# A four-layer graph network on one core: f1 rows by head in the encoder, more kept attention tiles, pair sums in tiles of their own

## Chip, core and metric

The kernel runs on one core of a Trainium2 chip. The metric is the device time in microseconds. An engine is named as the profile names it: PE is the matmul engine (PEld its weight loads), DVE the vector engine, ACT the engine of the activation functions, POOL the GpSimd engine, SP the engine that here only issues transfers. SP and ACT can issue transfers through the hardware queue, POOL through the software queue.

## What is computed

Four layers of a graph network over N = 2708 nodes with 512 features; each ends in a layer norm of its input plus its result. The change lies in the first layer (heads H = 4, width D = 128) and touches one product that the fourth layer uses. Of the reference:

```python
Xw = jnp.einsum('hnd,hde->hne', Xh, W)
f1 = jnp.einsum('hnd,hd->hn', Xw, V[:, 0, :, 0])
f2 = jnp.einsum('hnd,hd->hn', Xw, V[:, 1, :, 0])
sig = jax.nn.sigmoid(f1[:, :, None] + f2[:, None, :])
att = _masked_softmax(pattern[None] * sig, mask)      # local and long-range pattern are both adj
Xa = jnp.einsum('hij,hjd->hid', att, Xw)
Xn = _batchnorm(Xc, enc_bn_gamma, enc_bn_beta)
emb = _mlp_block(Xn, enc_mlp_W, enc_mlp_b, enc_mlp_bn_gamma, enc_mlp_bn_beta)
Y = jnp.einsum('hij,hjd->hid', att, Yh)               # Yh: emb by heads
Y = jnp.einsum('hnd,hed->hne', Y, W)
out = _mlp_block(jax.nn.elu(Yc), dec_mlp_W, ...)
```

The same attention matrix is thus used twice: on Xw (called the encoder here) and on emb (the decoder). Layer 2 needs the number of neighbours of each node. Layer 4 is a softmax attention with projections Wq and Wk; the kernel multiplies the two weight matrices once (called mqk) and applies the product.

## The kernel before

**Attention passes.** The attention matrix is never stored whole. `attention_pass` runs once for the encoder (`first` is true) and once for the decoder. It goes over two halves of the query nodes (`hf` 0 and 1, 1354 columns each) and, in each, over two pairs of heads (`p` 0 and 1): eight passes in all. A pass goes over the 22 blocks of 128 key nodes in the order `ORDER`; a block's number in that order is its place. The block with only 20 nodes stands at place 11.

**One step.** `form` makes the tile `t` (128 keys x 2 heads x 1354 queries) of a block: two tanh on ACT (L400), one for each head, from the row of f1 spread over all partitions (tile `f1b`) and the keys' f2 as bias; one operation on DVE that masks it with the adjacency block `a` (L408); one exponential on ACT (L409). PE then multiplies it with the values into six PSUM banks `po` (L478; a float32 matmul shows as two records, so a step has twelve). Tiles `t` have four buffers, adjacency blocks four in the encoder and three in the decoder.

**Encoder.** In passes with p = 0 the adjacency block is read from the input, changed so that missing edges become a large negative number (L389 and L390, with the single tile `z`), and written to `adj_d` from POOL (L394). All later passes read `adj_d`. The encoder also needs the sums of the exponentials over the keys: PE multiplies `t` with a block of ones into PSUM `psm` (L507). With p = 0, and at the first four and last two places, each tile is summed alone. At the other places with p = 1, DVE first adds the second tile of a pair to the first, in place (L498), and PE sums that. This is written as `add_up`, which is kept in `waiting` and called in the next step, before that step's matmuls; its add is ordered behind the next step's masking with `tc.issue_after`.

**Kept tiles.** The tiles at the places of `KEPT[p]` are written to memory by the encoder (L457, from POOL) and loaded by the decoder (L460, from SP) instead of being formed again.

**Counts.** For layer 2, `count` (L350, DVE) counts the missing edges of every block once in each half, in the decoder: with p = 0 where the block is formed there, with p = 1 where it is kept for p = 0. If a block is kept for both, it is loaded for the count alone. In `form` the count is written ahead of the tanh.

**f1 rows.** `f1b` holds both heads of a pass in one tile with two buffers, so the next pass's rows can be loaded while one runs (L427, SP).

**Between the passes.** At the end of a pass `finish` empties the six PSUM banks (encoder: copies L598 on ACT and DVE; decoder: `take`, L846 on DVE), and the rest of the work on the result is spread over the steps of the next pass.

**Weights of layer 4.** Between encoder and decoder, `merged(c)` makes block c of mqk with four matmuls of 512 columns (L699); two of the four blocks are made there, and the transposed weights go to memory. The other two are made after the decoder (L985, copied by L993, stored from POOL by L994), while the last batch norm is computed.

The text is not the order of the queues. The framework plans each engine's instructions by its own estimate of times, with the text's order as priority and `tc.issue_after(x)` as an edge to an instruction on the same engine.

## Time and profile before

| what | us |
|---|---|
| three runs | 3268.78, 3267.47, 3268.74 (median 3268.74) |
| the profiled execution | 3272.62 |
| its span, first to last instruction | 3270.8 |

In the profiled execution the first matmul of the eight passes starts at these times (us from the start of the span): encoder 44.4, 174.0, 298.6, 432.8; decoder 670.2, 778.4, 887.8, 1017.3. The encoder's last matmul ends at 556 and the decoder's last `po` matmul at 1121; between the two lie batch norm and MLP. Layer 2 of the reference starts with the first `tp_out` at 1186, its large product at 1277, and the two softmax layers take the span from 1493 on.

How to read it: the profile's lines give line, engine and tiles; a line "A <- B: x, n, y" of the waits says that A stood still x us in total, n times, at most y, until B was done. In the table by stretches each engine's busy time is followed by its number of instructions; then come the granted PE clock, the share of DMA time and GB/s. A busy PE can still run below its full rate, so the length of a step is to be compared too: twelve records of L478 take 4.55 us at full rate.

Rows of the groups that the change touches:

| operation | count, mean |
|---|---|
| L400 tanh, 1354 columns | 312, 1413 ns |
| L409 exponential, 2708 columns | 156, 2453 ns |
| L408 masking, 2708 columns | 156, 2976 ns |
| L498 pair add, 2708 columns | 14 whole ones, 2975 ns |
| L350 count, 1354 columns | 42 whole ones, 1560 ns |
| `a` from `adj_d` | 110 loads of 677 KB |
| `t` to and from memory | 16 stores and 16 loads of 1354 KB, besides those of the short block |
| `f1b` | 8 loads of 1354 KB |

### The profile page before, as it was taken

To read this page: it belongs to the slowest core of one execution; us is meant where nothing else is said; L and a number is where in the kernel's file an instruction comes from. 1 tells how busy PE (TensorE), PEld (TensorE's weight loads), DVE (VectorE), ACT (ScalarE), POOL (GpSimd) and SP (SyncE) were. 2 spreads that over 40 slices of the span, in tenths; PEclk is the share of its full clock that TensorE was granted. 3 is DMA by queue.
4 is the path that set the end of the run, shared out by engine and by line. 5 is a ranking of instruction groups with operands and counts; after the bars stand their busy time and mean duration, and the time that the engine had idled before them with its cause. 6 is when DMAs were issued, how large, how long until landed. Compare 5 with 4: busy or idle time off the path is not lost.

```text
span 3270.8 us, 30357 instructions
## 1 busy us (share of the span) xinstructions
PE 3212.9 (98%) x10906; PEld 1717.4 (53%) x10906; DVE 1944.1 (59%) x3144; ACT 1346.8 (41%) x1512; POOL 132.9 (4%) x215
## 2 busy tenths in 40 slices
PE   8999999999999999999999999999999999999999
PEld 5444444444444446885555555544455555555554
DVE  7878977867687685445136666777353442543433
ACT  6888886567868652001133434443021020110211
POOL 1100100000000000000010000000000000000000
PEclk9999999999999999999999999999999999999999
DMA  7856854245545412550034444553211111111100
GB/s 278 314 187 223 298 200 147 88 152 194 169 163 177 169 53 80 144 133 15 1 118 136 118 124 137 151 160 111 72 47 32 45 35 37 41 34 45 35 24 20
DMA packets 173158, 384.59 MB, mean 118 GB/s; under 512 B 21034, under 2 KB 115190, under 8 KB 168334
## 3 DMA queue, kind: packets, MB, share of 16 engines
q1 hardware_dynamic: 157214, 309.74, 31.1%
q0 software_dynamic: 15792, 72.91, 5.9%
q8 instruction: 86, 1.41, 0.2%
q14 instruction: 66, 0.54, 0.1%
HBM read 308.79 MB, written 73.24 MB: 117 GB/s over the span
## 4 chain that ended last, share of the span: by engine, by line
PE 87%; DVE 6%; ACT 3%; DMA 2%; issue 1%; SPq 0%; DVEq 0%; ACTq 0%
PE po L1377 23%; PE po L478 18%; PE ps_s L1256 17%; PE ps_nb L1109 7%; PE ps_wide L1158 4%; PE psm L507 3%; DVE t L408 2%; PE ps_hid L129 2%; PE ps_sup L1554 2%; PE ps_o L1485 2%; PE ps_dec L880 2%; ACT t L400 2%; ACT t L409 1%; PE ps_mlp L755 1%; DMA a<-adj_d 1%
## 5 line engine op out<-in xcount | busy, mean ns | idle before, releaser
L408 DVE SCALAR_TENSOR_TENSOR t<-t,a 128x2708 f32<-128x2708 f32 (+1 forms) x156 | 462.4, 2976 | 135.2 <-ACT t L400 131.2
L400 ACT ACTIVATE t<-f1b,f2h 128x1354 f32<-128x1354 f32 (+1 forms) x312 | 427.2, 1413 | 63.5 <-PE psm L507 32.1
L409 ACT ACTIVATE t<-t 128x2708 f32<-128x2708 f32 (+1 forms) x156 | 382.2, 2453 | 95.0 <-DVE t L408 94.8
L478 PE MATMUL po<-t,xw 128*128 128x452 f32 (+3 forms) x1056 | 412.9, 553 | 7.7 <-ACT t L409 7.7
L478 PE MATMUL po<-t,emb 128*128 128x452 f32 (+3 forms) x1056 | 403.1, 550 | 12.5 <-ACT t L409 9.2
L1256 PE MATMUL ps_s<-sup,hT 128*128 128x384 f32 (+1 forms) x1176 | 407.4, 490 | 0.0
L1377 PE MATMUL po<-sup,e 128*128 128x512 f32 x882 | 407.1, 595 | 0.2 <-DVE xs L1613 0.2
L1377 PE MATMUL po<-e,xs 128*128 128x384 f32 (+1 forms) x1176 | 406.0, 489 | 0.0
L1688 DVE SCALAR_TENSOR_TENSOR e<-a_cols,ps_s 128x384 f32<-128x384 f32 (+1 forms) x154 | 85.7, 556 | 450.4 <-PE ps_s L1256 427.5
L1256 PEld LDWEIGHTS ps_s<-sup,hT 128*128 128x128 f32 x1176 | 221.8, 190 | 164.2 <-issue 14.2
L478 PEld LDWEIGHTS po<-t,emb 128*128 128x128 f32 (+1 forms) x1056 | 194.9, 192 | 213.6 <-issue 189.2
L1377 PEld LDWEIGHTS po<-e,xs 128*128 128x128 f32 x1176 | 222.2, 190 | 160.2 <-issue 5.8
L478 PEld LDWEIGHTS po<-t,xw 128*128 128x128 f32 (+1 forms) x1056 | 189.1, 191 | 219.9 <-issue 199.9
L1377 PEld LDWEIGHTS po<-sup,e 128*128 128x128 f32 x882 | 160.3, 190 | 159.8 <-issue 136.9
L1256 PE MATMUL ps_s<-hT 128*128 128x384 f32 (+5 forms) x672 | 211.3, 461 | 1.4 <-DVE e L1604 0.8
L1355 ACT ACTIVATE e<-e 128x384 f32<-128x384 f32 (+1 forms) x308 | 151.9, 522 | 116.6 <-DVE e L1354 113.7
L1603 ACT ACTIVATE a_cols<-a_cols,neg_big 128x384 f32<-128x384 f32 (+1 forms) x154 | 94.5, 616 | 232.3 <-DMA a_cols<-in_adjT_dram 187.2
L1109 PE MATMUL ps_nb<-hid_hi,at 128*128 128x512 f32 x484 | 185.5, 390 | 0.4 <-DVE at L1101 0.4
L109 ACT ACTIVATE ln_rstd<-ln_rstd 128x1 f32<-128x1 f32 (+1 forms) x88 | 17.2, 201 | 395.9 <-DVE ln_rstd L108 395.4
L1109 PE MATMUL ps_nb<-hid_lo,at 128*128 128x512 f32 x462 | 180.1, 390 | 0.0
L1354 DVE TENSOR_TENSOR e<-e,nmax 128x384 f32<-128x384 f32 (+1 forms) x308 | 163.8, 555 | 23.3 <-ACT nmax L1347 23.3
L1256 PEld LDWEIGHTS ps_s<-hT 128*128 128x128 f32 x672 | 123.1, 190 | 90.2 <-issue 19.1
(252 smaller groups left out, 3321.0 us busy)
## 6 DMA issues: line engine op xcount, KB each, us to landing
a<-adj_d SPq DMA_DIRECT2D x110, 677.0 KB
a_cols<-in_adjT_dram SPq DMA_DIRECT2D x378, 192.0 KB
a<-in_adjT_dram SPq DMA_DIRECT2D x42, 677.0 KB
adj_d<-a POOLq DMA_DIRECT2D x42, 677.0 KB, 5.8
raw<-in_adjT_dram SPq DMA_DIRECT2D x105, 256.0 KB
kept<-t POOLq DMA_DIRECT2D x16, 1354.0 KB, 6.7
t<-kept SPq DMA_DIRECT2D x16, 1354.0 KB
a_cols<-in_adjT_dram SPq DMA_DIRECT2D x63, 202.0 KB
```

Source lines behind the costliest of these rows:

```text
L400: nc.scalar.activation(tv[:, k, :], f1b[:n, k, :w], AF.Tanh, bias=f2h[:n, jt, h : h + 1], scale=0.5,)
L408: step = nc.vector.scalar_tensor_tensor(tv, tv, GUARD, ab, ALU.add, ALU.mult)
L409: nc.scalar.activation(tv, tv, AF.Exp, scale=0.5)
L478: nc.tensor.matmul(po[HB * k + q][:, :qw], values[r : r + n, jt, h * P : (h + 1) * P], t[r : r + n, k, q0 : q0 + qw], start=(place == 0), ...
L507: nc.tensor.matmul(sums[k][32 * r : 32 * r + 32, :SW], ones32[:m], whole[:m, k, q0 + qw - SW : q0 + qw], start=first_one, stop=last_one,)
L1109: nc.tensor.matmul(pos[it][:n], at, half[:, jt, :], start=(jt == 0 and k == 0), stop=(jt == NT - 1),)
L1158: nc.tensor.matmul(ps[:, :width], w(c, o), xt(c), start=(c == 0), stop=(c == C - 1),)
L1256: nc.tensor.matmul(ps[:, b * P : w], keys[:, c, j0 : j0 + P], st["q"][:, c, b * P :], start=(c == 0), stop=(c == C - 1),)
L1354: nc.vector.tensor_tensor(e, e, st["nmax"][:, :w], ALU.add)
L1355: nc.scalar.activation(e, e, AF.Exp)
L1377: nc.tensor.matmul(out, lhsT, rhs, start=(k == 0), stop=(k == NT - 1))
L1603: nc.scalar.activation(a, a, AF.Identity, bias=neg_big[: a.shape[0]], scale=1.0e30)
```

## The change

Six things are changed. The words that go with the change speak of the decoder's f1 rows in tiles of two heads and of three adjacency buffers there; both are so in the kernel before as well, and stay.

1. `KEPT[1]` has eight places instead of five, so in each half three more tiles are stored by the encoder and loaded by the decoder. The places 4, 11 and 14 are now kept for both p; before, 11 alone.
2. `count` in `form` stands behind the exponential and is ordered behind the masking of its own step.
3. The pair sums: no `waiting`; the add follows its own step. It is made in two operations, one for each head, into tiles of their own ("z" and "pair", one buffer each). For the short block it is still made in place.
4. The encoder's f1 rows are in tiles of one head with three buffers. The second head's are loaded from ACT's queue.
5. `merged` makes three of four blocks between encoder and decoder, and one is left for after the decoder.
6. That last block is stored from SP instead of POOL.

```diff
-    KEPT = [(4, 8, 11, 14, 18), (3, 7, 11, 15, 19)]
+    KEPT = [(4, 8, 11, 14, 18), (1, 4, 7, 9, 11, 14, 17, 20)]
...
-    wqT_d = dram.tile([P, C, C // 2 * P], F32, name="wqT_d")
+    wqT_d = dram.tile([P, C, P], F32, name="wqT_d")
...
-            stage = att.tile([P, HP, HW], F32, tag="f1b", name="f1_rows", bufs=2)[:, 0, :]
-            f1b = att.tile([P, HP, HW], F32, tag="f1b", name="f1b", bufs=2)
+            stage, *f1b = [
+                att.tile([P, HW], F32, tag="f1b", name=name, bufs=HP + 1)
+                for name in ["f1_rows"] + ["f1b"] * HP
+            ]
...
-            spread = nc.sync.dma_start(
-                f1b[:, :, :w], f1_d[:HP, h0 : h0 + w].partition_broadcast(P)
-            )
+            for k in range(HP):
+                spread = nc.sync.dma_start(
+                    f1b[k][:, :w], f1_d[k, h0 : h0 + w].partition_broadcast(P)
+                )
...
-                if not first and p == (jt in KEPT[0]):
-                    count(hf, jt, att, a)
...
                 nc.scalar.activation(tv, tv, AF.Exp, scale=0.5)
+                if not first and p == (jt in KEPT[0]):
+
+                    with tc.issue_after(step.ins):
+                        count(hf, jt, att, a)
                 return step
...
-                        f1b = att.tile([P, HP, HW], F32, tag="f1b", name="f1b", bufs=2)
...
+                        if first:
+
+                            f1b = [
+                                att.tile([P, HW], F32, tag="f1b", name="f1b", bufs=HP + 1)
+                                for k in range(HP)
+                            ]
+                            with early:
+                                nc.sync.dma_start(f1b[0][:, :w], f1[:, 0, :])
+                            nc.scalar.dma_start(f1b[1][:, :w], f1[:, 1, :])
+                        else:
+                            both = att.tile([P, HP, HW], F32, tag="f1b", name="f1b", bufs=2)
+                            f1b = [both[:, k, :] for k in range(HP)]
+                            with early:
+                                nc.sync.dma_start(both[:, :, :w], f1)
...
-                        if waiting is not None:
-                            waiting(step)
-                            waiting = None
...
-                            if more is not None:
-                                with tc.issue_after(behind.ins):
-                                    nc.vector.tensor_tensor(
-                                        whole[: more.shape[0], :, :w],
-                                        whole[: more.shape[0], :, :w],
-                                        more,
-                                        ALU.add,
-                                    )
...
-                            waiting = partial(add_up, before, P, tv, False, False)
+                            whole, m = [], P
+                            for k, tag in enumerate(("z", "pair")):
+                                both = att.tile([P, HW], F32, tag=tag, name="pair", bufs=1)
+                                nc.vector.tensor_tensor(
+                                    both[:, :w], before[:, k, :w], tv[:, k, :], ALU.add
+                                )
+                                whole.append(both)
...
-            nc.gpsimd.dma_start(wqT_d, wqT[:, :, half * P :])
-            merged(1)
+            nc.gpsimd.dma_start(wqT_d, wqT[:, :, (C - 1) * P :])
+            for c in range(1, C - 1):
+                merged(c)
...
-                    for c in range(half):
-                        for o in range(C):
-                            nc.tensor.matmul(
-                                po[1 + c],
-                                wq_again[:, o, c * P : (c + 1) * P],
...
+                    for o in range(C):
+                        nc.tensor.matmul(
+                            po[1],
+                            wq_again[:, o, :],
...
-                for c in range(half):
-                    nc.scalar.activation(mqk[:, c, :], po[1 + c], AF.Copy, scale=qscale)
-                    nc.gpsimd.dma_start(
-                        mqk_d[:, :, half + c, :].rearrange("o p i -> p o i"),
+                nc.scalar.activation(mqk, po[1], AF.Copy, scale=qscale)
+                nc.sync.dma_start(
+                    mqk_d[:, :, C - 1, :].rearrange("o p i -> p o i"),
```

## The prediction

> **What bounds the kernel now.** I read the engine totals first, then the stretches by stage, then the waits of the two attention stretches, and last the chain and the PE timeline around the longest PE stalls.
>
> ```profile
> PE 3212.9 (98%) x10906; PEld 1717.4 (53%) x10906; DVE 1944.1 (59%) x3144; ACT 1346.8 (41%) x1512; POOL 132.9 (4%) x215
> ...
> 204.00:356.00 152.00, 147.98 (x623) 65.12 (x622) 134.10 (x83) 133.24 (x82) 10.65 (x19) 0.99 0.64 225
> ...
> 566.00:676.00 110.00, 106.50 (x335) 51.21 (x334) 89.06 (x140) 48.93 (x63) 2.92 (x4) 1.00 0.27 94
> 676.00:790.00 114.00, 106.12 (x286) 52.09 (x286) 74.50 (x59) 88.93 (x58) 1.06 (x2) 0.97 0.56 190
> 790.00:890.00 100.00, 96.17 (x258) 47.16 (x257) 65.68 (x45) 82.77 (x54) 0.00 (x0) 0.98 0.52 173
> 890.00:1000.00 110.00, 110.00 (x294) 54.46 (x293) 90.55 (x95) 74.89 (x55) 0.00 (x0) 0.98 0.48 165
> ```
>
> PE is the bound: 98% of the span and in no stage far from full. In the decoder all of 890 to 1000 is PE work. So an edit that relieves ACT, DVE or DMA is worth only what PE stands still for their sake, and an edit that moves PE work is worth what stands still where it left and where it arrives. Now those standstills, waits of ACT, DVE and PE, encoder (180 to 305, then PE in 180 to 556) and decoder (670 to 1121):
>
> ```profile
> ACT t L400 <- PE psm L507: 6.6, 4, 2.6
> ...
> PE po L478 <- ACT t L409: 7.7, 8, 2.3
> PE psm L507 <- DVE t L498: 2.8, 2, 1.4
> ...
> DVE z L350 <- DMA a<-adj_d: 30.1, 13, 4.2
> ...
> ACT t L409 <- DVE t L408: 71.0, 39, 5.8
> ...
> PE po L478 <- ACT t L409: 9.2, 7, 5.8
> PE po L478 <- DVE ot L846: 3.1, 1, 3.1
> ```
>
> The decoder chain is: DVE's zero count L350 stands ahead of a masking L408 whose tanh is done, and waits 30.1 us in all for its adjacency block; ACT's exponentials wait 71.0 us for L408; PE waits 9.2 us for ACT and 3.1 us for the DVE copies L846. Nearly all of that PE wait is at two changes of pass. The first of them in the chain of waits, then the PE timeline of both:
>
> ```profile
> 767.36 3.92 DMA a<-adj_d
> ...
> 771.40 0.12 DVE z L350
> ...
> 772.97 2.90 DVE t L408
> ...
> 775.90 2.47 ACT t L409
> ```
>
> ```profile
> 778.40 7.82 PE L478 MATMUL po<-t,emb 128*128 128x452 f32 x12 [5.80 <-ACT t L409]
> ...
> 887.75 8.51 PE L478 MATMUL po<-t,emb 128*128 128x452 f32 x14 [3.14 <-DVE ot L846]
> ```
>
> The reader is to see the count's wait for its load, the masking behind it, the exponential behind that, and PE last. A step of twelve matmul records takes 4.55 us in the chain where PE is full (14 take 5.31), so these two steps are also 3.3 and 3.2 us slow after the gap. The two changes of pass cost 5.80 + 3.3 + 3.14 + 3.2 = 15.4 us; the rest of the decoder's PE waits is 12.3 - 8.9 = 3.4 us.
>
> **The skill.** "TensorE: Matmul & The Clock Gate", What's actually happening: an idle window of about 3.4 us halves the PE clock, about as long a busy one restores it. The trace agrees: 7.82 instead of 4.82 us right after the 5.80 us gap, while a 1.42 us gap in the encoder is not followed by slow records. "VectorE: DVE Perf Modes", the TRN2 errata section: an fp32 tensor_tensor takes (N + 151)/0.96 ns. For N = 2708 that is 2978 ns; the trace has 2974 for L498. For 1354 it is an estimate of 1568 ns (the nearest row, L390 over 1354, has 1569). "DMA: Bandwidth & Descriptors", Issuing engines are not separate DMA queues: another issuing engine saves issue time only. Here POOL spends 0.77 us on one L994 issue, SP about 0.35 on one of its own.
>
> **The change, part by part** (against the profiled execution, 3272.62 us with a span of 3270.8; it is 3.88 above the median 3268.74, so I subtract the sum from the median).
>
> *Counts behind the masking.* The 44 counts stay (1.56 us each), so nothing is removed. Those made inside `form` now follow their own L408, whose wait for the block they share: the 30.1 us of DVE waits on blocks for tiles further on go, but for six counts of tiles that are kept in both passes (two now), which load a block for themselves. The price is that a block is freed 1.56 us later. With three blocks and 5.3 us a step (2 x 1.41 tanh + 2.45 exp on ACT) a block has three steps, 15.8 us, for a 4 us load, 2.98 masking and 1.56 count, 8.5 us: covered.
>
> *Kept tiles in p = 1, five to eight a half.* Six tiles fewer to form in the decoder: 6 x 5.28 = 31.7 us of ACT and 6 x 2.98 = 17.9 us of DVE go, none of it on the path while PE is full, but the places 1 and 20 lie at the two changes of pass, where it is. Adjacency loads go from 35 to 34 a half (p = 0 gets two more, p = 1 three fewer), kept loads from 10 to 13: 6 x 1354 - 2 x 677 KB = 6.8 MB over some 450 us, 15 GB/s beside 165 to 190. These are on SP's one queue, where a kept load that waits for a tile holds up the adjacency loads behind it; with 14 formed steps in 22 there is time. Six more stores of 1354 KB in the encoder, 0.53 us of POOL each, hold their tile 6.7 us after the exponential; a tile is wanted again after four steps.
> For both parts together: of 15.4 us at the changes I take 10 (a gap under about 2 us would not slow the clock), of the other 3.4 one: -11. Bounds: 0 (the wait moves from L350 to L408 on the same loads) and -18.
>
> *Pair sums in tiles of their own.* Each half of the encoder has eight pairs in p = 1. Before, the sums on PE read a `t` tile, which is free only after them (ACT t <- psm, 6.6 us in one pass). Now DVE adds into tiles "z" and "pair", and both `t` are free after the add. PE work is the same. PE idles 7.7 + 2.8 = 10.5 us here, of which 8.2 lie in p = 1 (1.41 + 0.47 + 1.42 + 0.60, and the same with 0.41 more in the second half). DVE pays 2 x 1.57 instead of 2.97, 16 x 0.16 = 2.6 us, beside PE. The add is no longer ordered behind the next masking and the sums no longer held back a step. Ends of the exponential at 0: next masking may run to 2.98, adds to 6.1, own po matmuls on PE to 4.55; if PE has no lead it waits 1.6 us per pair. Taken: -4.5; bounds -8 and +25 (16 x 1.6, the slower rival).
>
> *f1 rows by head in the encoder, three tiles.* One tile is free for the next pass, the second head's only after the last tanh of head 0. In the change at 173 us that tanh ends at 163.5 and the next pass reads head 1 at 174.3, 10.7 us later; the 1354 KB load of the start took from 24.30 to 32.65, so half of it is an estimate of 4 to 5 us, and 0.4 us to issue on ACT, in front of tanhs. Hidden at p = 0 to 1; less slack at p = 1 to 0. The first load is split, and head 0 is there earlier, but DVE then waits at 35.06 for an adjacency block. Also "z" is now busy in p = 1, so preparing the next half starts some 6 us later than 279.7 and still ends before its step at 298.6. Taken +0.5, bounds -1.5 and +5. The decoder's f1 tiles of two heads and its three blocks are as before: nothing.
>
> *One product of the query and key weights moved from the end to before the MLP.* Eight matmul records of 0.43 us (16 of L985 take 7.03): 3.4 us of PE leave the end and come to 580 us. There PE is full but for 3.5 us in 566 to 676, and the product's PSUM buffer is free only when L720 ends at 579.7. Bounds +1.0 and +3.4; taken +2.6. A copy (0.6 us ACT) comes along. At the end, PE stands idle from 1184.3 to 1186.1 after L985 anyway; the chain runs over bn_shift, four L1036 on ACT and one L993 of 0.49 us before PE's transposes. One of two L993 goes: -0.5. The store now leaves from SP earlier than 1186.3; its landing at 1189.05 stands shortly before L1019 and L1029, after which PE starts at 1191.08. SP has the b1 load and raw blocks behind the store; the b1 load waited for it already (34.1 us, SP's waits). Bounds 0 and -2.6; taken -1.2.
>
> Sum: -11 - 4.5 + 0.5 + 2.6 - 1.2 = -13.6; I leave 1.6 for small new stalls, since the order in each queue comes from the framework's planning and not from the text: -12. 3268.74 - 12 = 3257.
>
> **Rivals.** (A) The above, 3257, chance 0.55.
> (B) The waits only change their name: adjacency loads are late for L408 as they were for L350, and DVE is as late with L846. For it speaks that loads leave when a block is freed, now later. Against it: 15.8 us against 8.5. Decoder -3, encoder -2, moved product +2.6, end -1.2: -3.6, 3265. Chance 0.22.
> (C) All PE stalls of both stretches go: -18 - 8 + 1 - 1 = -26, 3243. Against it: the partial tile at place 11 takes PE under 2 us and ACT 5.3, so some gap stays. Chance 0.10.
> (D) Slower: PE's sums wait for the adds. In its queue the sums stand in front of the next step's po; 16 pairs x 1.6 = 25, and the encoder's -4.5 is lost: -11 + 25 + 0.5 + 2.6 - 1.2 = +16, 3285. It decides from 1.0 us a pair on (about +6.5 in all). For it: psm already waited 2.8 us for L498. Against: ACT mostly runs the next tanh pair before the exponential, so the masking is over when the exponential ends, and PE usually has a lead. Chance 0.13.
>
> **How the numbers follow.** A difference under 0.2% (6.5 us) can't be told from no change. A lies mostly beyond it (0.51 of 0.55), with C 0.10 and a quarter of B 0.05: faster 0.66. The rest of A and most of B: same 0.20. D and a little of B: slower 0.14. Range: half of C and all but D's upper part fall off, 3245 to 3274; A alone 3250 to 3263.
>
> **What would show it.** Right: in the decoder no DVE wait of L350 on a block but in the few counts of doubly kept tiles; PE gaps at the two changes under 2 us each, their first steps at 4.8 us; ACT no longer waiting for psm in the encoder; some 3 us more PE work between 566 and 590. Wrong: L408 waiting for blocks as long as L350 did (B); psm waiting for L498's successor by over 1 us a pair (D); ACT waiting for f1b at a change of pass; SP held on kept loads with PE behind it.

## The result, and the profile after

| | kernel before | kernel after |
|---|---|---|
| median | 3268.76 (3267.47 to 3269.73) | 3248.76 (3247.06 to 3254.93) |
| profiled execution | 3272.62 | 3254.93 |
| its span | 3270.8 | 3253.1 |

The ratio after to before is 0.9942, 95% interval 0.9927 to 0.9957. The kernel is 20 us faster. The forecast was 12 us faster, 3257 with a range of 3245 to 3274: direction and range held, and the gain was larger.

To see where the time came from, I cut each trace at the first matmul of each attention pass (the "mid" stretch runs from the encoder's last matmul to the decoder's first, the "end" stretch from the decoder's last attention matmul to the first `ps_hid` matmul of the next layer). The second column of the kernel after is a second execution of it, experiment 1.

| stretch, us | before | after | after, once more |
|---|---|---|---|
| up to the first pass | 44.4 | 42.4 | 44.1 |
| encoder passes | 129.6, 124.6, 134.2, 123.5 | 129.6, 122.2, 138.8, 123.6 | 129.8, 123.6, 132.3, 123.6 |
| mid | 113.9 | 115.4 | 115.3 |
| decoder passes | 108.2, 109.4, 129.6, 103.5 | 100.2, 105.5, 128.1, 102.2 | 100.2, 105.5, 127.9, 102.2 |
| end | 70.2 | 65.7 | 65.7 |
| all the rest | 2079.7 | 2079.4 | 2078.9 |

Of the 21.5 us between the spans 3270.8 and 3249.3, the decoder brought 14.8, the end 4.5, the encoder 2.5, the rest 0.8 and the start 0.3; the mid stretch took 1.4. The encoder's third pass of the first profile, 138.8, is that execution's: it was 132.3 in the next (why is shown further down).

Engine totals of the kernel after, from the page, and then the stretches by engine, cut at its own decoder passes (columns: stretch, length, busy PE, PEld, DVE, ACT and POOL with counts, granted clock, DMA share, GB/s):

```profile
PE 3210.1 (99%) x10906; PEld 1718.6 (53%) x10906; DVE 1924.7 (59%) x3152; ACT 1317.7 (41%) x1494; POOL 136.3 (4%) x219
```

```profile
672.00:772.00 100.00, 99.53 (x280) 49.34 (x280) 71.33 (x63) 78.33 (x53) 1.06 (x2) 1.00 0.61 206
772.00:878.00 106.00, 102.69 (x278) 50.90 (x278) 64.35 (x48) 81.63 (x54) 0.00 (x0) 1.00 0.57 203
```

PE has the same work, and in the first decoder pass it stands still for half a microsecond in all; the second still has 3.3. The waits of the decoder, kernel after (waiter, releaser: total us, times, longest):

```profile
DVE z L352 <- DMA a<-adj_d: 2.0, 1, 2.0
...
ACT t L409 <- DVE t L408: 61.1, 36, 3.9
...
PE po L491 <- ACT t L409: 3.8, 2, 3.3
```

The zero counts' waits for adjacency blocks are down to 2.0 us, and no wait of the masking L408 for a block is listed at all. ACT still waits 61 us for L408; only one of PE's longer waits (3.3 us) is put down to ACT, and experiments 9 and 10 show that even there another wait decided. Here are the two changes of pass on PE, kernel after (start, duration, then the idle time ahead in brackets):

```profile
763.68 14.00 PE L491 MATMUL po<-t,emb 128*128 128x452 f32 x36
...
877.67 6.39 PE L491 MATMUL po<-t,emb 128*128 128x452 f32 x12 [3.31 <-ACT t L409]
```

At the first change (the second pass begins at 772.1 inside the first of these lines) there is no gap any more. At the second there is one of 3.31 us, as long as before (3.14), with the twelve matmuls behind it at 6.39 instead of 4.82.

In the encoder between 180 and 556 us ACT no longer waits for the pair sums so long (12.4 us where it was 24.7 over the same stretch), but it waits for stores of kept tiles, and the sum of PE's own waits has hardly changed (7.7 and 2.8 before):

```profile
ACT t L400 <- PE psm L524: 12.4, 13, 3.0
...
ACT t L400 <- DMA kept<-t: 8.6, 5, 4.7
```

```profile
PE po L491 <- ACT t L409: 7.2, 6, 2.4
PE psm L524 <- DVE t L509: 2.8, 2, 1.4
```

The longest of those waits for a store reached PE in this execution. ACT and PE, kernel after:

```profile
354.05 1.43 ACT L400 ACTIVATE t<-f1b,f2h 128x1354 f32<-128x1354 f32 x1 [4.67 <-DMA kept<-t]
...
355.38 2.45 ACT L409 ACTIVATE t<-t 128x2708 f32<-128x2708 f32 x1
...
357.88 6.51 PE L491 MATMUL po<-t,xw 128*128 128x452 f32 x12 [2.20 <-ACT t L409]
```

The tanh of place 12 needs the tile of place 8, whose store took 9.6 us to land; the exponential of place 10 stands behind that tanh in ACT's queue, and PE waits 2.20 us for it. In the second execution the same store took 6.9 us, the tanh waited 1.30 us, and PE had no gap there.

### The profile page after: what moved, and what is told of

Read it like the earlier page. It is cut to its first block, busy times and chain, and to the rows that moved or that the text cites. A ratio compares the mean times of both kernels' runs of the same rounds, so it can differ in the third digit from the quotient of the medians.

```text
span 3253.1 us, 30379 instructions
## 1 busy us (share of the span) xinstructions
PE 3210.1 (99%) x10906; PEld 1718.6 (53%) x10906; DVE 1924.7 (59%) x3152; ACT 1317.7 (41%) x1494; POOL 136.3 (4%) x219
## 3 DMA queue, kind: packets, MB, share of 16 engines
q8 instruction: 86, 1.41, 0.2%
## 4 chain that ended last, share of the span: by engine, by line
PE 83%; issue 9%; DVE 3%; ACT 2%; DMA 1%; POOL 1%; SPq 0%; POOLq 0%; DVEq 0%; ACTq 0%
PE po L1385 23%; PE ps_s L1264 18%; PE po L491 15%; PE ps_nb L1117 7%; PE ps_wide L1166 4%; PE ps_hid L128 2%; PE ps_sup L1562 2%; PE ps_o L1493 2%; PE ps_dec L893 2%; PE ps_mlp L768 1%; PE psm L524 1%; ACT t L400 1%; ACT t L409 1%; PE ps_s L1256 1%; DVE t L408 1%
## 5 line engine op out<-in xcount | busy, mean ns | idle before, releaser
L408 DVE SCALAR_TENSOR_TENSOR t<-t,a 128x2708 f32<-128x2708 f32 (+1 forms) x150 | 444.5, 2975 | 154.1 <-ACT t L400 149.4
L400 ACT ACTIVATE t<-f1b,f2h 128x1354 f32<-128x1354 f32 (+1 forms) x300 | 411.4, 1413 | 65.6 <-PE po L491 33.3
L409 ACT ACTIVATE t<-t 128x2708 f32<-128x2708 f32 (+1 forms) x150 | 367.5, 2454 | 95.8 <-DVE t L408 95.6
L1264 PEld LDWEIGHTS ps_s<-sup,hT 128*128 128x128 f32 x1176 | 221.8, 190 | 164.2 <-issue 14.2
```

The costliest lines, as they stand in the source:

```text
L400: nc.scalar.activation(tv[:, k, :], f1b[k][:n, :w], AF.Tanh, bias=f2h[:n, jt, h : h + 1], scale=0.5,)
L408: step = nc.vector.scalar_tensor_tensor(tv, tv, GUARD, ab, ALU.add, ALU.mult)
L409: nc.scalar.activation(tv, tv, AF.Exp, scale=0.5)
L1264: nc.tensor.matmul(ps[:, b * P : w], keys[:, c, j0 : j0 + P], st["q"][:, c, b * P :], start=(c == 0), stop=(c == C - 1),)
```

## The experiments

My theory for the larger part: the counts behind the masking and the three more kept tiles free the decoder at the changes of pass. Rivals: one of the two alone does it; the number of kept tiles does it and not their places; f1 by head or the pair sums have a share. For the end: one product less, or the other queue for its store. Where an experiment is timed, its own runs of the kernel before stand beside it (medians 3270.17, 3271.21, 3270.52 and 3267.78 in the four groups).

**1. The kernel after once more.** No edit.

> The changed kernel once more, nothing edited, to see how far its profile and time vary. In its first profile the decoder's four passes took 436.0 us (450.7 before), the stretch from the last po matmul to the first ps_hid matmul 65.8 (70.2 before), the third encoder pass 138.8 (134.2 before), and that run was the slowest of four (3254.9 beside 3247 to 3249). If the third pass's 4.6 us belong to the kernel, they are there again and the time is 3248 to 3249 all the same; if they were that one execution's, the third pass takes about 134.3 here. The decoder and the end are as in the first profile, within 1 us.

Measured 3251.05 (3247.68 to 3255.48), ratio 0.9944 [0.9932, 0.9957]. The stretches are in the table above. The gain repeats, and so do the decoder's passes, to 0.2 us.

**2. Counts ahead again**, with the eight kept tiles.

```diff
+                if not first and p == (jt in KEPT[0]):
+                    count(hf, jt, att, a)
+
                 for k in range(HP):
...
-                if not first and p == (jt in KEPT[0]):
-
-                    with tc.issue_after(step.ins):
-                        count(hf, jt, att, a)
```

> The changed kernel with the counts written ahead of the tanh again, as before; all else stays. Theory order (the counts that waited for their block were what held up the masking): DVE waits on blocks at the count come back to 20 us or more, the PE gap at the first change of pass in the decoder comes back, and the time is 3255 to 3259. Theory kept (three more kept tiles a half took the load off the changes of pass): the decoder stays within 2 us of 436.0 and the time within 2 us of the changed kernel.

Measured 3267.23 (3263.03 to 3270.51), ratio 0.9991 [0.9985, 0.9998]; decoder 450.3 us, as in the kernel before (450.7). Three more kept tiles a half without the move of the counts bring nothing to the decoder. Its DVE waits:

```profile
DVE z L352 <- DMA a<-adj_d: 20.7, 10, 4.3
```

**3. Five kept tiles again**, with the counts behind.

```diff
-    KEPT = [(4, 8, 11, 14, 18), (1, 4, 7, 9, 11, 14, 17, 20)]
+    KEPT = [(4, 8, 11, 14, 18), (3, 7, 11, 15, 19)]
```

> The changed kernel with five kept tiles for p = 1, as before; all else stays. Theory order: the decoder loses at most 3 us, 3249 to 3252. Theory kept: the gaps at the changes of pass come back, decoder 444 to 450 us, time 3256 to 3262. In either case six stores fewer in the encoder: if those hold tiles up there, ACT's waits on stores of kept tiles go (11 us in the first profile) and the encoder gains 1 to 3 us.

Measured 3258.23 (3255.38 to 3261.02), ratio 0.9965 [0.9952, 0.9977]; decoder 446.7. The counts' waits on blocks are gone here, and still the first change of pass has a gap:

```profile
775.02 5.43 PE L491 MATMUL po<-t,emb 128*128 128x452 f32 x10 [6.36 <-ACT t L409]
```

The name behind the arrow is not what held PE; experiments 9 and 10 show that. So taking the counts' waits away is worth 4.0 us of the decoder by itself (450.7 to 446.7), the tiles 0.4, and both 14.8: most of it needs the two together.

**4. Two blocks of the weight product at the end again** (both stored from POOL, as before).

```diff
-            for c in range(1, C - 1):
-                merged(c)
+            merged(1)
...
+                    for c in range(half):
```

> The changed kernel with two of four weight products made before the MLP and two after the decoder, stored from POOL, as before; all else stays. Theory end: 3.4 us of PE work leave the full stretch at 580 us (encoder's end to the decoder's first po 1.4 to 2.6 us shorter), and the end, from the last po matmul to the first ps_hid, is 70 us again instead of 65.8; time +2 to +3 us against the changed kernel. Rival: the end was shorter for other reasons (what the decoder left to do), so it stays at 66 and the kernel is 1.5 to 2.5 us faster than the changed one.

Measured 3252.36 (3248.66 to 3254.27), ratio 0.9946 [0.9932, 0.9959]; mid 112.3 (115.3 with the product there), end 70.3 (65.7). What the moved product costs in the middle and what it brings at the end nearly cancel: 4.6 - 3.0 = 1.6 us of gain, which the times can't tell from nothing.

**5. Five kept tiles, two of them at the changes of pass.**

```diff
-    KEPT = [(4, 8, 11, 14, 18), (1, 4, 7, 9, 11, 14, 17, 20)]
+    KEPT = [(4, 8, 11, 14, 18), (1, 7, 11, 15, 20)]
```

> The kernel after with five kept tiles in the decoder's second pair of heads, as before the change, but at places 1, 7, 11, 15 and 20: two of the five lie at the changes of pass. With five tiles at 3, 7, 11, 15 and 19 the decoder's four passes took 446.7 us, with eight at 1, 4, 7, 9, 11, 14, 17 and 20 they took 435.9. If what the eight tiles bring is that no masking stands at place 1 ahead of the eviction of the pass before, the decoder takes 436 to 439 us here, PE has no gap at the first change of pass (near 775 us), and the whole is 3250 to 3254. If it is the number of tiles that VectorE need not mask and ScalarE need not form (three more, twice), the decoder stays at 444 to 447 and the whole at 3256 to 3260.

Measured 3253.29 (3251.41 to 3254.61), ratio 0.9947 [0.9934, 0.9959]; decoder passes 100.6, 108.3, 128.1, 103.7, in all 440.8. It falls between the two forecasts: the places bring the first pass's 6.3 us (106.9 to 100.6), the other three tiles 4.9 us in the passes with p = 1 (108.3 to 105.5, 103.7 to 102.2) and around them.

**6. Pair sums in place again**, behind the next masking.

```diff
+                        if waiting is not None:
+                            waiting(step)
+                            waiting = None
...
-                            for k, tag in enumerate(("z", "pair")):
-                                both = att.tile([P, HW], F32, tag=tag, name="pair", bufs=1)
...
+                            waiting = partial(add_up, before, P, tv, False, False)
```

> The kernel after with the encoder's pair sums as before: added into the first of the two score tiles, one addition for both heads, behind the masking of the next tile. If the sums in tiles of their own brought the encoder's 2.4 us (511.8 before, 509.4 in the second run of the kernel after), the encoder's four passes take 511 to 513 here and the whole is 2 to 3 us above the kernel after, with PE's waits for VectorE's sums and ScalarE's waits for score buffers back to those of before. If the encoder's difference comes from elsewhere (the start, f1 by head, the counts), the encoder stays at 509 to 510 and the whole stays within 1 us of the kernel after.

Measured 3253.26 (3251.87 to 3256.79), ratio 0.9950 [0.9937, 0.9962]; encoder 512.4, decoder 436.0. That is 2.2 to 4.5 us above the medians of the kernel after (3248.76, 3251.05) and of experiment 7 (3249.99), and the encoder's 3 us is of the same size, but the intervals overlap. The profiles of the other experiments help: in the three with sums in place (the kernel before, this one and experiment 12) the encoder took 510.5 to 512.4, and in ten of the eleven with tiles of their own 504.0 to 510.0, the eleventh being the first profile with its long store (514.2). With eight kept tiles alone it is 510.5 and 512.4 against 507.7 to 509.9. A gain of some 2 us by the pair tiles is thus well supported; how much it is within 1 to 4 us stays open.

**7. The last block's store from POOL.**

```diff
-                nc.sync.dma_start(
+                nc.gpsimd.dma_start(
                     mqk_d[:, :, C - 1, :].rearrange("o p i -> p o i"),
```

> The kernel after with one edit: the store of the one weight-product block that is left at the end of the decoder is issued by GpSimd, as the two were before, not by SyncE. The stretch from the decoder's last attention matmul to the first of the next stage was 70.3 us before and 65.7 after. If the issuing queue is what made it shorter (the store then lands earlier, and with it the memset and the copy that wait for its tile), it goes back to 69 to 70 here and the whole rises by 3 to 5 us. If it is that one block less is computed and copied by ScalarE, the stretch stays at 65 to 67 and the whole within 1.5 us.

Measured 3249.99 (3247.71 to 3252.18), ratio 0.9937 [0.9924, 0.9951]; end 65.7, to the tenth as from SP. The queue is not it; the second product is. Its place in the kernel before, ACT, PE, POOL and DVE in order of time:

```profile
1182.83 2.73 ACT L1036 ACTIVATE ot<-ot,bn_shift,bn_scale 128x452 f32<-128x452 f32 x4 [0.84 <-DVE bn_shift L558]
...
1185.46 0.57 ACT L993 ACTIVATE wq_again<-po 128x512 f32<-128x512 f32 x1
...
1186.09 1.10 PE L1049 MATMUL tp_out<-ident,ot 128*128 128x128 f32 x8 [1.75 <-ACT wq_again L993]
1186.32 0.77 POOL L994 DMA_DIRECT2D mqk_d<-wq_again  x1 [3.70 <-ACT wq_again L993]
...
1189.46 0.48 DVE L1019 MEMSET hid_hi<- 128x512 f32 x1
...
1191.08 1.22 PE L129 MATMUL ps_hid<-w_sb,ot 128*128 128x512 f32 x1 [3.90 <-DVE ln_rstd L110]
```

and the same steps in the kernel after:

```profile
1169.89 5.35 ACT L1044 ACTIVATE ot<-ot,bn_shift,bn_scale 128x452 f32<-128x452 f32 x8 [0.84 <-DVE bn_shift L570]
...
1171.37 1.34 PE L1057 MATMUL tp_out<-ident,ot 128*128 128x128 f32 x4 [3.40 <-DVE ot L1051]
...
1172.03 0.48 DVE L1027 MEMSET hid_hi<- 128x512 f32 x1
...
1173.65 2.08 PE L128 MATMUL ps_hid<-w_sb,ot 128*128 128x512 f32 x2 [0.93 <-DVE w_sb L1037]
```

Before, four of ACT's shifts stand ahead of the second copy L993, and PE's transposes start when it ends, though the first of their input was ready at 1184.25. From there two things run side by side up to the memset at 1189.46: the store issued behind the copy lands at 1189.05, and DVE's queue is busy until 1189.41 with the statistics of the transposed rows and two additions. The second ended last, by 0.36 us, so the trace does not tell whether the landing alone would have held the memset as long (in experiment 4, with two products again, the two ended within 0.1 us of each other). In the kernel after the store lands at 1170.93, and the memset again follows DVE's own work, at 1172.03. From the first shift to the first `ps_hid` matmul it is 8.25 us before and 3.76 after: 4.5 us less, the whole difference of the stretch.

**8. Place 1 kept for the first pair of heads too.**

```diff
-    KEPT = [(4, 8, 11, 14, 18), (1, 4, 7, 9, 11, 14, 17, 20)]
+    KEPT = [(1, 8, 11, 14, 18), (1, 4, 7, 9, 11, 14, 17, 20)]
```

> The kernel after with the kept tiles of the first pair of heads at places 1, 8, 11, 14 and 18 in place of 4, 8, 11, 14 and 18, so that place 1 is a kept tile in every decoder pass. What is left in the kernel after is a PE gap of 3.3 us at the second change of pass (near 876 us), behind a masking of that pass's tile at place 1, and 12 us of matmuls at a lower clock behind it. If the place rule holds, this gap goes, the decoder's second or third pass is 3 to 6 us shorter, and the whole is 3245 to 3249. If the stall at the second change is due to something else (the f1 row, the kept tile's load, the half's change), the decoder stays at 436 and the whole within 1.5 us of the kernel after; the count of place 1 in the first pair of heads, which loads its block by itself, could then cost 1 to 3 us.

Measured 3251.38 (3250.17 to 3256.55), ratio 0.9947 [0.9934, 0.9959]; decoder 438.3, 2.4 more than the kernel after. My rule "place 1" failed at the second change (what ran at a lower clock there in the kernel after was twelve matmuls of 6.39 us, not the 12 us of the expectation). But the gap there has changed its name. PE, then DVE:

```profile
871.28 7.84 PE L491 MATMUL po<-t,emb 128*128 128x452 f32 x12 [3.85 <-DVE ot L859]
```

```profile
865.77 2.98 DVE L408 SCALAR_TENSOR_TENSOR t<-t,a 128x2708 f32<-128x2708 f32 x1 [2.07 <-ACT t L400]
868.67 3.66 DVE L859 SCALAR_TENSOR_TENSOR ot<-po,bn_scale,rb 128x452 f32<-128x452 f32 x6
```

The releaser is not the Exp but L859, the `take` that empties PSUM. Six of them stand in DVE's queue behind a masking that waits 2.07 us for its tanh. It is that of place 2: with place 1 kept, the next tile to be formed has moved up into its position. That led to the next three.

**9. and 10. Place 1 alone, place 20 alone** (five kept tiles).

```diff
-    KEPT = [(4, 8, 11, 14, 18), (1, 4, 7, 9, 11, 14, 17, 20)]
+    KEPT = [(4, 8, 11, 14, 18), (1, 7, 11, 15, 19)]
```
```diff
-    KEPT = [(4, 8, 11, 14, 18), (1, 4, 7, 9, 11, 14, 17, 20)]
+    KEPT = [(4, 8, 11, 14, 18), (3, 7, 11, 15, 20)]
```

> The kernel after with the second pair's kept tiles at places 1, 7, 11, 15 and 19: five, with place 1 but without place 20. The decoder's four passes took 446.7 us with five tiles at 3, 7, 11, 15, 19 and 440.8 with five at 1, 7, 11, 15, 20; nearly all of the difference was in the first pass (106.9 against 100.6), which ends with the first matmul of the next. If place 1 alone does it, the first pass takes 100 to 101 here and the decoder 440 to 442. If the tile at place 20 is what clears the end of the pass for the change, the first pass stays near 107 and the decoder at 445 to 447.

> The kernel after with the second pair's kept tiles at places 3, 7, 11, 15 and 20: five, with place 20 but without place 1. If place 1 is what the first change of pass needs, the first pass takes 106 to 108 us here, with a PE gap of 5 to 6 us at its end, and the decoder 444 to 448. If place 20 does it, the first pass takes 100 to 102 and the decoder 440 to 442. For the second change of pass, which place 20 stands just ahead of, theory has no number: a gap of 5 us in both five-tile kernels says that it changes nothing there.

Measured: place 1 alone 3252.82 (3248.60 to 3256.14), ratio 0.9944 [0.9931, 0.9956], first pass 100.5, decoder 440.6; place 20 alone 3259.76 (3254.87 to 3262.46), ratio 0.9966 [0.9955, 0.9978], first pass 107.1, decoder 447.7. Place 1 does it, place 20 does nothing. DVE at that change, first with place 20 alone:

```profile
756.60 2.97 DVE L408 SCALAR_TENSOR_TENSOR t<-t,a 128x2708 f32<-128x2708 f32 x1
763.42 2.98 DVE L408 SCALAR_TENSOR_TENSOR t<-t,a 128x2708 f32<-128x2708 f32 x1 [3.84 <-ACT t L400]
766.32 3.66 DVE L859 SCALAR_TENSOR_TENSOR ot<-po,bn_scale,rb 128x452 f32<-128x452 f32 x6
```

then with place 1 alone:

```profile
756.17 2.98 DVE L408 SCALAR_TENSOR_TENSOR t<-t,a 128x2708 f32<-128x2708 f32 x1
760.65 3.66 DVE L859 SCALAR_TENSOR_TENSOR ot<-po,bn_scale,rb 128x452 f32<-128x452 f32 x6 [1.51 <-PE po L491]
```

and PE, place 20 alone:

```profile
757.75 4.82 PE L491 MATMUL po<-t,emb 128*128 128x452 f32 x12 [0.15 <-ACT t L409]
768.93 2.60 PE L491 MATMUL po<-t,emb 128*128 128x452 f32 x3 [6.36 <-ACT t L409]
```

The masking at 756 is that of the next pass's place 0 in both. With place 20 alone the masking of place 1 follows it in DVE's queue, ahead of the six takes, and waits 3.84 us for its tanh, although the pass's last matmul ends at 762.57 and the results in PSUM are then ready. With place 1 kept there is nothing to mask, and the takes run while PE is still in the pass's last step. The name of the releaser on PE misleads. PE's first matmul needs a PSUM tile that holds both heads of the first columns, so both of its takes must be done. Here the takes go through one head and then the other, and the second of the two is take four: it ends at 768.78, and PE starts 0.15 us later. The Exp that is named ended at about the same time, but it belongs to place 1, which these first matmuls don't read; that of place 0 had ended at 762.07. In experiment 8 the Exp of the next formed tile even ends after PE has started (871.30 and 871.28), and there too take four had ended 0.15 us before. The distance is the same at the other gaps: take four ends at 778.25 and PE starts at 778.40 at the first change of the kernel before, 877.52 and 877.67 at the one left in the kernel after. Where both heads of the first columns are taken first, take two decides: 887.61 and 887.75 at the second change of the kernel before. The order of the takes differs from change to change; from the ends of takes two and four it is worth an estimated 1.2 us where PE waits for them.

DVE's timeline at the first change shows the same in the other kernels. In the kernel before, the count, the masking of place 1 and the takes:

```profile
771.40 1.57 DVE L350 TENSOR_SCALAR_CACHE_REDUCE z<-a 128x1354 uint8<-128x1354 f32 x1 [4.06 <-DMA a<-adj_d]
...
772.89 2.98 DVE L408 SCALAR_TENSOR_TENSOR t<-t,a 128x2708 f32<-128x2708 f32 x1
775.78 3.66 DVE L846 SCALAR_TENSOR_TENSOR ot<-po,bn_scale,rb 128x452 f32<-128x452 f32 x6
```

In the kernel after, the masking of place 0, the takes, the masking of place 2:

```profile
765.80 2.97 DVE L408 SCALAR_TENSOR_TENSOR t<-t,a 128x2708 f32<-128x2708 f32 x1
770.71 3.66 DVE L859 SCALAR_TENSOR_TENSOR ot<-po,bn_scale,rb 128x452 f32<-128x452 f32 x6 [1.94 <-PE po L491]
...
775.48 2.97 DVE L408 SCALAR_TENSOR_TENSOR t<-t,a 128x2708 f32<-128x2708 f32 x1
```

In experiment 2, with the same tiles kept, the masking of place 2 and then the takes:

```profile
771.02 2.98 DVE L411 SCALAR_TENSOR_TENSOR t<-t,a 128x2708 f32<-128x2708 f32 x1 [5.16 <-ACT t L403]
773.92 3.66 DVE L858 SCALAR_TENSOR_TENSOR ot<-po,bn_scale,rb 128x452 f32<-128x452 f32 x6
```

With the counts ahead, the masking of place 2 stands ahead of the takes, even with place 1 kept, and PE has a gap of 6.20 us there. This is how the eight tiles can bring nothing without the move of the counts. So what matters is not place 1 as such but that no masking of a second tile stands ahead of the takes. Why the framework's planning puts it there in one kernel and not in the other, these runs don't show. The direct test, an edge that orders the second tile's masking behind the takes, was not run; the encoder has such an edge (`taken`, from its copies to the forming of place 2), the decoder has none.

**11. Place 0 kept for the first pair of heads**, a sixth tile.

```diff
-    KEPT = [(4, 8, 11, 14, 18), (1, 4, 7, 9, 11, 14, 17, 20)]
+    KEPT = [(0, 4, 8, 11, 14, 18), (1, 4, 7, 9, 11, 14, 17, 20)]
```

> The kernel after with a sixth kept tile of the first pair, at place 0: places 0, 4, 8, 11, 14 and 18. In the kernel after the one gap left in the decoder is at the second change of pass: the third pass's first matmul waits 3.3 us for the Exp of that pass's tile at place 0, and 12 matmuls after it run at a lower clock. With the tile of place 0 loaded instead of formed, this wait goes: the second pass takes 101 to 103 us instead of 105.5, the decoder 431 to 434, and the whole falls by 2 to 5 us to 3245 to 3249, less what the encoder pays for one more stored tile in its first and third passes (0 to 3 us). If the first matmul then waits for the next tile's Exp or for the eviction instead, the decoder stays within 2 us of 436.

Measured 3248.01 (3245.13 to 3250.13), ratio 0.9930 [0.9917, 0.9942]; decoder passes 100.2, 103.4, 126.5, 102.2, in all 432.3, 3.6 us less than in the kernel after, with one gap left:

```profile
872.75 5.57 PE L491 MATMUL po<-t,emb 128*128 128x452 f32 x14 [1.16 <-DVE ot L859]
```

Here too a masking stands ahead of the takes, with its count, but both are over when the pass's last matmul ends (871.59). The gap is 2.2 us shorter than in the kernel after (an estimated 1.2 of it because take two decides, not four), and no slow matmuls follow it. It is the lowest median of all kernels here. Its interval meets that of the kernel after, so that it is faster than that one is shown by the trace's decoder, not by the times.

**12. The kernel before with the two decoder parts alone**: eight kept tiles, counts behind the masking.

```diff
-    KEPT = [(4, 8, 11, 14, 18), (3, 7, 11, 15, 19)]
+    KEPT = [(4, 8, 11, 14, 18), (1, 4, 7, 9, 11, 14, 17, 20)]
...
-                if not first and p == (jt in KEPT[0]):
-                    count(hf, jt, att, a)
...
+                if not first and p == (jt in KEPT[0]):
+
+                    with tc.issue_after(step.ins):
+                        count(hf, jt, att, a)
```

> The kernel before with two parts of the change alone: the eight kept tiles at 1, 4, 7, 9, 11, 14, 17 and 20, and the counts behind the masking. If the decoder's 14.8 us come from these two and from nothing else of the change (f1 by head, pair sums in tiles of their own, the moved weight product), the decoder's four passes take 435 to 437 us here as in the whole change, with the stretch after them at 70 and the one ahead of them at 112 to 114 as before, and the whole is 3253 to 3258. If f1 by head has a share of it, the decoder stays above 439. A whole under 3252 would say that the other three parts together bring nothing.

Measured 3254.58 (3252.46 to 3257.11), ratio 0.9958 [0.9945, 0.9972]; decoder 436.1, mid 112.4, end 70.2. The decoder's gain is these two parts and nothing else of the change. What is left of the whole change, 4.6 to 6.9 us by the ratios of the kernel after and of experiment 7 (0.9944 to 0.9937), lies outside the decoder.

## Why the prediction came out as it did

The range and the direction held. The likeliest case had the right places and, but for its last link, the right mechanism. Four of its terms were off in size: two were too small by 3.8 and 3.3 us, one too large by some 2 us, and the discount was not needed. So the forecast of 12 us came out too small, though within its range. Term by term, against the second execution of the kernel after:

*Counts behind the masking and kept tiles together, -11: it was -14.8.* Of the 15.4 us at the two changes I took 10. The 15.4 itself is a little high: 3.3 and 3.2 us of slow matmuls came from setting lengths of the timeline (7.82 and 8.51) against steps of the chain (4.55 and 5.31). Like with like, 7.82 - 4.82, the first is 3.0, and from the granted clock it is 3.1 and 3.0, so 15.0 in all. The first change lost its 8.9 us wholly; the second kept a gap of 3.31 us and 1.6 us of slow matmuls instead of 3.14 and 3.0. That is 10.1, as taken. The term that was mis-sized is the other 3.4 us of PE waits, of which I let one go: 0.5 us is left, so 2.9 went. The remaining 1.8 us I can't place; they lie mostly in the three passes in which PE's gaps became fewer. Of the sign that the gaps at both changes fall under 2 us, only the first change showed it. That "places 1 and 20 lie at the two changes" was half right: place 1 counts, place 20 doesn't (experiments 9 and 10). And the chain I showed, from the count's load over masking and exponential to PE, named the wrong last link: PE waited for the takes queued behind that masking. That the size for the changes came out right all the same is luck in part: the exponential and take four happened to end together, at 778.36 and 778.25. The bound "0, the wait moves from L350 to L408 on the same loads" did not occur.

*Pair sums in tiles of their own, -4.5: about -2.* Encoder 511.8 to 509.4, and 512.4 with the sums put back; experiment 6 has the scatter. I had counted 8.2 us of PE's waits in p = 1 as those the change could touch. But 2.8 of them, the two waits for L498, belong to the short block, whose addition stays in place: they are still there as L509, 1.41 us each. Of the waits for the exponential, those of the first half (0.47, 1.42 and 0.60) became one of 2.38 us in the second execution, behind five tanhs that ACT runs in a row (6.67 us), and PE was slow behind it. The waits were gathered, not removed. A sign that I had named for being right, that ACT no longer waits for `psm`, came only by half (24.7 us to 12.4 and 14.2). The rival in which PE's sums wait for the additions did not happen: PE's only such waits are the old ones.

*f1 rows by head, +0.5.* No wait for `f1b` stands among those of the encoder or the decoder; a cost of this size can't be seen apart. Experiment 12 shows that it has no share in the decoder.

*Product moved ahead of the decoder, +2.6.* Mid 113.9 to 115.3 against the kernel before, 112.3 to 115.3 with the edit alone: +1.4 to +3.0, as bounded. Over all profiles it is 112.3, 112.4 and 113.9 without the product and 114.5 to 117.5 with it.

*The end, -1.2 with bounds 0 and -2.6: it was -4.5, outside them.* I priced the second copy's own 0.49 us and the landing by how closely it stood before the memset. What fell was the whole delay that the second product causes: the four shifts in front of its copy, and behind it PE's transposes with DVE's work on them, and the store. The first store of the kernel before landed at 1184.58, the second at 1189.05, 4.47 us later, which is near the 4.5, but DVE's queue, not the landing, ended last (experiment 7). The step that failed is to price the removal of a link by its own duration where all that it holds up moves forward.

*Discount of 1.6 for new stalls.* The only new one of that sort that I found is ACT's wait for stores of kept tiles in the encoder: 8.6 us in the first profile, where PE stood 2.20 us for one of them, and 6.4 us in the second, where PE didn't feel it (1.5 us in the kernel before). The store that PE felt is one of those that the kernel before makes too. The discount took the forecast the wrong way.

Sum of the terms: -13.6 forecast, -21.5 measured between those two spans, -20 in the medians.

## What to carry to other kernels

Where accumulators have one buffer, look at what stands in the evicting engine's queue ahead of the eviction at each change of pass: one prepared tile too many, waiting for its own input, held the matmul engine here for most of its wait and work (a gap of 6.4 us for 3.84 + 2.98). When a step is taken out of a serial stretch, price it by how much earlier its last consumer can start, not by its own duration: follow everything that waits for it, and here also the queue in front of that consumer. Two edits of which one alone brings 4.0 us and the other 0.4, but both 14.8, are one condition in two halves; try such edits together before dropping either.

## What the runs showed of the hardware that I had not expected

**The clock after a gap.** How PE runs after a gap isn't told by the gap's length, and my "a gap under about 2 us would not slow the clock" has no support. Already in the kernel before, a gap of 1.42 us was followed by full pace, and one of 1.41 us by 16 matmuls that took 2.16 us instead of 1.35. The granted clock tells more. In all fourteen profiles it drops to half for 3.41 us or twice that (the last time is cut off by the end of the span), and the starts within one execution are whole multiples of 3.413 us apart. Here are windows of that length, with the granted clock as the third figure from the end; first the second execution of the kernel after:

```profile
249.46:252.87 3.41, 1.03 (x6) 0.49 (x3) 3.41 (x2) 3.41 (x3) 0.55 (x1) 1.00 0.63 205
252.87:256.28 3.41, 3.41 (x6) 1.69 (x5) 3.41 (x3) 3.41 (x3) 0.00 (x0) 0.50 1.00 265
```

then experiment 6:

```profile
274.29:277.70 3.41, 1.82 (x5) 0.57 (x3) 3.41 (x3) 1.86 (x2) 0.00 (x0) 1.00 0.18 25
277.70:281.11 3.41, 2.44 (x7) 1.31 (x8) 3.41 (x2) 3.41 (x3) 0.53 (x1) 1.00 0.92 375
```

In the first, a gap of 2.38 us lies whole in one window, and the next window is at half clock. In the second, a gap of 2.56 us is split between two windows, 1.59 and 0.97 us, and the clock stays. "TensorE: Matmul & The Clock Gate", What's actually happening, in the Trainium skill says that the window is free-running and about 3.4 us long, and the traces agree. That a whole window must be idle, as the page says too, doesn't fit: 2.38 us of 3.41 were enough, and in the second execution of the kernel after even 0.96 us, in a window of which 1.35 us were matmuls of 20 rows (how such matmuls count is not shown). A window at half clock in which PE is busy throughout costs half of 3.41 us, 1.7: the twelve matmuls behind that gap of 0.96 us took 6.51 us, 1.7 more than 4.82.

**Two more.**

- The same program's encoder pass took 138.8 us in one execution and 132.3 in the next, while its decoder passes agreed to 0.2 us. The two traces place 6.2 of these 6.5 us: PE stood 3.1 us longer (2.20 of them for the store shown above), and the half clock cost it 4.8 us instead of 1.7. A difference of a few microseconds in such a stretch needs more than one profile.
- Issuing a 256 KB store from POOL takes 0.79 us and from SP 0.37, and here it made no difference to anything after it: the memset behind it was waiting for DVE's own queue, which was busy 0.35 us past the landing.
